# Two-pass scores on exact halves, rotary products shared between VectorE and GpSimd, and a range test by sums of squares, in a latent attention kernel

## The chip, the cores and the metric

The kernel runs on one core of one Trainium2 chip, in one launch. The metric is the device time in microseconds (us), the median of the runs; lower is better. Engines are named as in the profile: PE is TensorE (PEld its weight loads), DVE is VectorE, ACT is ScalarE, POOL is GpSimd, SP is SyncE, which here only issues DMAs.

## The reference, cut to what matters

Eight sequences (batches) of 1024 rows with 256 features go through a layer of latent attention and then through two layers of windowed attention with an MLP. The change touches the first layer alone. There are 16 heads of 16 dimensions; a rotary term of 32 dimensions is shared by all heads.

```python
c_kv = x @ W_kv_down
k_rope = _rotary_apply(c_kv @ W_k_rope, cos, sin)
k = (c_kv @ W_k_up).reshape(Bb, Tt, NH, HD)
v = (c_kv @ W_v_up).reshape(Bb, Tt, NH, HD)
q = (x @ W_q).reshape(Bb, Tt, NH, HD)
q_rope = _rotary_apply(x @ W_q_rope, cos, sin)
scores = jnp.einsum('bqhd,bkhd->bhqk', q, k)
scores = scores + jnp.einsum('bqr,bkr->bqk', q_rope, k_rope)[:, None]
scores = scores / scale
scores = jnp.where(causal[None, None], -jnp.inf, scores)
w = jax.nn.softmax(scores, axis=-1)
attn = jnp.einsum('bhqk,bkhd->bqhd', w, v).reshape(Bb, Tt, D_MODEL)
return attn @ W_o
```

The input x is normalised first, and the result is added to it. All data are float32.

## The kernel before, in words

The kernel has two stages. `mla` computes the first layer for the eight batches and leaves its result in DRAM (`x2d`); `local` computes the rest. A test at the end (`Verdict`) looks whether all values stayed in the range in which the short cuts of the kernel are exact; if not, a general version runs (it doesn't run here).

The exponential of the scores is split: exp(q k + rotary) = exp(q k) * exp(rotary). The rotary factor `er` is the same for all heads, so it is computed once for a block of queries and keys (`rotary`, L402 to L414), and each head's exp(q k) is multiplied by it (`turned`, L441 to L451).

Work in `mla` goes by units. A batch has 36 of them (list `units`, L571 to L577). A unit covers 512 columns for four heads, which is a block of 128 keys (or two narrower blocks at the causal border) for up to 512 queries c (c = 1 the later half of the queries, c = 0 the earlier) and a group g of four heads. For each unit:

- `scores` (L421): for each of the four heads a matmul over 32 rows of the array: `self.k[g]` (four heads of 32 rows) against `self.q`. Only 16 rows of 32 belong to one head: q holds two heads in 32 rows, and k is multiplied by a mask in `keys` (L372), so that the other head's rows are zero. The four matmuls lie in four row groups of the array. They fill two tiles `sc` in PSUM, and ACT takes the exponentials to two tiles `pt` of 128x1024 (L437), of six buffers.
- `turned` (L451): DVE multiplies both `pt` by `er`, which is broadcast over the heads.
- `values` (L453): four matmuls in four column groups add up v^T pt, with a column of ones in v for the sums; at the end of a row of units ACT copies the sum out, and `finished` and `turn_back` transpose and divide on DVE.

The order on PE, DVE, ACT and POOL is written out by hand (`manual_schedule`, L586 to L618). Step s issues the scores of unit s, the products of unit s - 1, the values of unit s - 2, and then the side work that the table `beside` (L513 to L556) gives to step s: for the same batch, the next one (1), the one after it (2) or the one before (-1). Side work is the projections of the next batch (`query`, `keys`, `value`, `down`, `rope_q`, `rope_k`), its normalisation and transposes, the rotary blocks and the output (`out_add`). A projection is summed by `dense` in one of two banks of PSUM (L324) and then copied out by ACT. Each engine works through its own list in order, so an instruction that waits holds up all behind it on the same engine. SP's order is not in the hand-written list: it issues loads of x, stores of x2d and, in the second stage, many DMAs.

`query` (L355) multiplies by wq, `keys` (L362) by wk; both are copies of the weights with columns put in the order in which two heads lie in 32 rows (L241 to L256). `rotary` takes two exponentials of each block, exp(+s) into `er` and exp(-s) back into PSUM, each with its sum along the row (`most`, `least`), for the range test at L620 to L623. A block at the causal border is cut to its triangle by POOL (L411). `rsqrt` (L125), a power on POOL, is the only other work of POOL in this stage.

In the second stage POOL works all the time: two operations of 128x1024 (L873 and L879) for each window, and selects. L956 and L1147 are DVE operations with two operands in SBUF.

Of the kernel before, what the change touches and what calls it, by code (L numbers as in the profile page):

```python
# [28 lines left out]

F32 = mybir.dt.float32  # L30
AF = mybir.ActivationFunctionType
ALU = mybir.AluOpType
AX = mybir.AxisListType
PSUM = bass.MemoryType.PSUM

P = 128
D = 256
T = 1024
# [15 lines left out]
TURN = 1e17  # L54
# [27 lines left out]
def preln_mla_local_kernel(  # L82
# [72 lines left out]
    def mla(ctx: ExitStack, verdict):  # L155
# [21 lines left out]
        def bank(name):  # L177
            if shared is None:
                return psum.tile([P, 512], F32, tag="mm", name=name)
            return two_banks(name)[:, 0, :]  # L180
# [59 lines left out]

        wq = wp.tile([P, 2, 2, 4, 2, HD], F32, name="wq")  # L241
        wk = wp.tile([P, 2, 4, 2, HD], F32, name="wk")
        mask = wp.tile([P, 2], F32, name="mask")
        for e in range(2):
            nc.vector.tensor_reduce(
                mask[:, e : e + 1], ident.rearrange("p (r e d) -> p r e d", e=2, d=HD)[:, :, e, :], AX.XY, ALU.add
            )
        for m in range(2):
            for e in range(2):
                cols = slice(128 * m + 64 * e, 128 * m + 64 * e + 64)  # L250
                nc.scalar.copy(
                    wq[:, :, m, :, e, :], wqnat[:, :, cols].rearrange("p c (r d) -> p c r d", d=HD)
                )
                nc.scalar.copy(wk[:, m, :, e, :], wknat[:, cols].rearrange("p (r d) -> p r d", d=HD))
        wq = wq.rearrange("p c m r e d -> p c m (r e d)")
        wk = wk.rearrange("p m r e d -> p m (r e d)")  # L256

        vs = []  # L260
# [7 lines left out]

        most = wp.tile([P, B * 12], F32, name="most")
        least = wp.tile([P, B * 12], F32, name="least")  # L270

        class Batch:


            def __init__(self, b):
                self.b = b
                self.sums = {}

# [23 lines left out]
            def normalise(self, n, part):  # L302
                mv, rstd = self.found[n]
                if part == 0:
                    if n == 0:
                        self.xn = []
                    self.xn.append(p1.tile([P, 4, D], F32, tag="xn", name=f"xn{self.b}_{n}", bufs=3))
                xn = self.xn[n]
                for i in (2 * part, 2 * part + 1):
                    nc.vector.tensor_scalar(  # L310
                        xn[:, i, :], self.x[:, 4 * n + i, :], mv[:, i, 0:1], rstd[:, i : i + 1],
                        ALU.subtract, ALU.mult,
                    )
# [34 lines left out]
            def rope_k(self, n, part=None):  # L348
# [3 lines left out]
                if ps is not None:  # L352
                    nc.vector.tensor_tensor(self.rk[:, HALF[n]], ps, tab[:, 1, HALF[n]], ALU.mult)

            def query(self, m, n, c, part=None):  # L355
                if m == 0 and n == 1 and c == 0 and not part:
                    self.q = of[self.b % 2].tile([P, 2, T], F32, tag="q", name=f"q{self.b}")
                ps = self.dense(f"psq{m}_", [wq[:, 0, m, :], wq[:, 1, m, :]], self.xnc, n, c, part)
                if ps is not None:
                    on_a(self.q[:, m, HALF[n]], ps)  # L360

            def keys(self, m, n, part=None):  # L362

                if n == 0 and not part:
                    if m == 0:
                        self.k = []
                    for e in range(2):
                        g = 2 * m + e
                        self.k.append(of[self.b % 2].tile([P, T], F32, tag=f"k{g}", name=f"k{self.b}_{g}"))
                ps = self.dense(f"psk{m}_", [wk[:, m, :]], [self.ckvT], n, 0, part)  # L370
                for e in range(2) if ps is not None else ():
                    nc.scalar.activation(  # L372
                        self.k[2 * m + e][:, HALF[n]], ps, AF.Identity, scale=mask[:, e : e + 1]
                    )

            def value(self, g, part=None):
# [25 lines left out]
            def rotary(self, c, kb):  # L402
                q0, w, er = self.block(c, kb)
                ps = bank(f"psR{self.b}_{c}_{kb}")
                times(ps[:, :w], self.rk[:, kb * P : (kb + 1) * P], self.rq[:, q0 : q0 + w], True, True)
                n = 12 * self.b + 8 * (1 - c) + kb
                nc.scalar.activation(er, ps[:, :w], AF.Exp, scale=SCALE, accum_out=most[:, n : n + 1])  # L407

                nc.scalar.activation(ps[:, :w], ps[:, :w], AF.Exp, scale=-SCALE, accum_out=least[:, n : n + 1])
                if q0 == kb * P:  # L410
                    nc.gpsimd.affine_select(  # L411
                        out=er[:, :P], in_=er[:, :P], pattern=[[1, P]],
                        compare_op=ALU.is_ge, fill=0.0, base=0, channel_multiplier=-1,
                    )  # L414

            def start(self):
# [4 lines left out]
            def scores(self, key, parts):  # L421
# [3 lines left out]
                for c, g, kb in parts:  # L425
                    q0, w, _ = self.block(c, kb)
                    for n in range(4):
                        rows = slice(32 * n, 32 * n + 32)
                        nc.tensor.matmul(  # L429
                            two[n // 2][:, n % 2, lo : lo + w], self.k[g][rows, kb * P : (kb + 1) * P],  # L430
                            self.q[rows, g // 2, q0 : q0 + w], start=True, stop=True,
                        )
                    lo += w
# [7 lines left out]
            def turned(self, parts, pts):  # L441
# [6 lines left out]
                er = er.unsqueeze(1)  # L448
                for pt in pts:
                    t = pt.rearrange("p j (s w) -> p (j s) w", w=w)  # L450
                    nc.vector.tensor_tensor(t, t, er.to_broadcast([P, 1024 // w, w]), ALU.mult)  # L451

# [21 lines left out]
            def finished(self, c, g, oT):  # L474


                nat = late.tile([P, 16, 32], F32, tag="onat", name=f"onat{self.b}_{c}_{g}", bufs=3)
                nc.vector.transpose(nat.rearrange("p b d -> p (b d)"), oT)
# [39 lines left out]
        for step, who, *what in (  # L518
# [21 lines left out]
            (21, 1, "rope_k", 1), (21, 1, "query", 0, 1, 0, 0),  # L540
            (22, 1, "query", 0, 1, 0, 1), (22, 1, "query", 0, 1, 1),
            (23, 1, "keys", 0, 0), (23, 2, "statistics", 0, 0),
            (24, 1, "value", 0),
            (25, 1, "value", 1),
            (26, 1, "keys", 0, 1), (26, 2, "statistics", 0, 1),
            (27, 1, "rotary", 1, 0),
# [72 lines left out]

        ok = small.tile([P, 2, B * 12], F32, tag="okr", name="okr", bufs=1)  # L620
        nc.vector.tensor_scalar(ok[:, 0, :], most, TURN, None, ALU.is_le)
        nc.vector.tensor_scalar(ok[:, 1, :], least, TURN, None, ALU.is_le)
        verdict.add(ok.rearrange("p m n -> p (m n)"), "turn")  # L623

# [1215 lines left out]
```

## Time and profile before

| What | us |
|---|---|
| median of three runs (3347.45 to 3350.44) | 3350.26 |
| the profiled execution, first to last instruction (span) | 3347.4 |
| first stores of x2d, batches 0 to 4 | 151.58, 272.93, 394.25, 515.59, 636.92 |
| last copy of a sum in the first stage (ACT, L78) | 1011.2 |
| one rotary product on DVE (128x1024, L451) | 1.217 |
| one exponential of scores on ACT (128x1024, L437) | 1.029 |
| busy in 272.9 to 394.3: PE, DVE, ACT, POOL | 120.4, 107.8, 96.9, 9.5 |
| mean granted clock of PE | 0.993 of full |

In the profile a group is one source line on one engine: out<-in with the names of tiles, then count, busy time, mean ns of one, and the idle time of the engine just before, with who ended it. An fp32 matmul leaves two records, each with its weight load. The chain of waits follows the work that ended last backwards. In a timeline each line has start, length, engine, source line, operation and count. Two operations that follow each other on DVE or ACT overlap by some hundredths of a microsecond, so that busy time is a little less than count times mean.

### The profile page before, as it was taken

How to read it: one execution, taken by the hardware profiler on the slowest of the kernel's cores; microseconds unless marked ns; L12 is line 12 of the kernel's file. 1: busy time of each engine (PE TensorE's matmuls, PEld its weight loads, DVE VectorE, ACT ScalarE, POOL GpSimd, SP SyncE). 2: the span in 40 equal slices, each digit the busy share in tenths (PEclk: the TensorE clock that was granted, in tenths of full speed). 3: DMA queues.
4: the chain of work that ended last, by engine and by line, in shares of the span. 5: the costliest groups of instructions: out<-in, count | busy, mean ns of one | idle time of the engine just before them, and what ended most of it. 6: DMA issues, size and time to landing. Idle time of an engine off the chain costs nothing.

```text
span 3347.4 us, 79461 instructions
## 1 busy us (share of the span) xinstructions
PE 3270.7 (98%) x33826; PEld 1777.5 (53%) x33826; DVE 2686.0 (80%) x3993; ACT 1713.1 (51%) x2238; POOL 1341.6 (40%) x1031
## 2 busy tenths in 40 slices
PE   8999999999987899999999999999999999999998
PEld 2433333333333556666565666566666566665665
DVE  5888888888897887888878887777878778787773
ACT  6878878877862244434444434444444444344441
POOL 1000000000006655655655555555555555555540
PEclk9999999999998899999999999999999999999999
DMA  1000000000032444445344354444545444454431
GB/s 63 8 20 27 8 20 27 8 20 14 14 105 81 115 114 120 123 115 143 105 121 127 113 136 130 137 127 136 134 134 139 121 126 130 124 148 119 109 107 58
DMA packets 369290, 311.74 MB, mean 93 GB/s; under 512 B 154607, under 2 KB 333214, under 8 KB 368798
## 3 DMA queue, kind: packets, MB, share of 16 engines
q1 hardware_dynamic: 366942, 304.16, 33.1%
q8 instruction: 268, 4.39, 0.6%
q10 hardware_dynamic: 1984, 2.41, 0.2%
q14 instruction: 96, 0.79, 0.1%
HBM read 165.96 MB, written 140.51 MB: 92 GB/s over the span
## 4 chain that ended last, share of the span: by engine, by line
PE 90%; DVE 3%; ACT 2%; DMA 1%; issue 1%; SPq 1%; POOL 1%; ACTq 0%; DVEq 0%
PE ag L1088 17%; PE pair L859 13%; PE sc L429 9%; PE psy L1129 8%; PE acc L462 8%; PE psw L1005 7%; PE o L972 6%; PE pv L886 6%; PE pair L931 4%; PE psq L200 2%; PE psx L200 2%; PE s L980 2%; PE psR L200 2%; DVE pt L451 1%; PE psy L1135 1%
## 5 line engine op out<-in xcount | busy, mean ns | idle before, releaser
L451 DVE TENSOR_TENSOR pt<-pt,er 128x1024 f32<-128x1024 f32 x576 | 674.8, 1217 | 77.8 <-ACT pt L437 77.8
L437 ACT ACTIVATE pt<-sc 128x1024 f32<-128x1024 f32 x576 | 560.7, 1029 | 174.0 <-PE sc L429 161.6
L1088 PE MATMUL ag<-d,l 128*128 128x512 f32 x1408 | 640.4, 597 | 1.2 <-DVE xs L1009 0.8
L873 POOL TENSOR_TENSOR t<-t,t 128x1024 f32<-128x1024 f32 x128 | 302.0, 2360 | 792.0 <-DVE t L869 792.0
L937 ACT ACT_TABLE_LOAD x120 | 154.0, 1283 | 702.0 <-PE pair L931 702.0
L859 PE MATMUL pair<-l_qkv,xT 128*128 128x512 f32 x1024 | 469.2, 601 | 5.5 <-DMA xT<-zx 2.4
L1088 PEld LDWEIGHTS ag<-d,l 128*128 128x128 f32 x1408 | 262.2, 190 | 310.2 <-issue 278.1
L125 POOL TENSOR_TENSOR rn<-ss,half 128x16 f32<-128x16 f32 x128 | 373.4, 2917 | 13.7
L429 PE MATMUL sc<-q,k 32*128 32x512 f32 (+3 forms) x3072 | 369.9, 522 | 5.1 <-ACT pt L437 5.0
L462 PE MATMUL acc<-pt,v 128*32 128x512 f32 (+3 forms) x3072 | 332.9, 496 | 4.8 <-DVE pt L451 4.6
L859 PEld LDWEIGHTS pair<-l_qkv,xT 128*128 128x128 f32 x1024 | 193.7, 192 | 248.8 <-issue 207.6
L864 ACT ACTIVATE sq<-pair 128x1024 f32<-128x1024 f32 x128 | 131.0, 1023 | 333.2 <-issue 269.1
L866 DVE TENSOR_TENSOR t<-pair,l_cos 128x1024 f32<-128x1024 f32 x128 | 156.2, 1220 | 157.4 <-ACT sq L864 156.7
L1129 PE MATMUL psy<-l,hid 128*128 128x256 f32 x1280 | 281.5, 379 | 0.0
L1101 DVE SCALAR_TENSOR_TENSOR hid<-ag,l_b,ge 128x512 f32<-128x512 f32 x160 | 115.9, 724 | 196.3 <-ACT ge L1100 171.3
L1129 PEld LDWEIGHTS psy<-l,hid 128*128 128x128 f32 x1280 | 243.2, 190 | 46.7 <-issue 15.1
L937 ACT ACTIVATE pt<-pair 128x1024 f32<-128x1024 f32 (+1 forms) x256 | 234.9, 968 | 56.7 <-PE pair L931 55.4
L429 PEld LDWEIGHTS sc<-q,k 32*128 32x128 f32 x3072 | 157.3, 184 | 199.9 <-ACT pt L437 154.3
L411 POOL TENSOR_SCALAR_AFFINE_SELECT er<-er 128x128 f32<-128x128 f32 x64 | 51.5, 804 | 524.0 <-ACT er L407 524.0
L879 POOL TENSOR_TENSOR t<-t,rn 128x1024 f32<-128x1024 f32 x128 | 249.2, 1947 | 10.0
L972 PEld LDWEIGHTS o<-pt,v 128*32 128x32 f32 x7680 | 201.6, 110 | 88.0 <-issue 82.0
L886 PE MATMUL pv<-l_qkv,xT 128*128 128x512 f32 x512 | 240.6, 592 | 0.0
(132 smaller groups left out, 4876.8 us busy)
## 6 DMA issues: line engine op xcount, KB each, us to landing
z<-turned SPq DMA_DIRECT2D x512, 128.0 KB, 2.4
qkT<-z SPq DMA_DIRECT2D x128, 512.0 KB, 3.7
y<-xs SPq DMA_DIRECT2D x128, 128.0 KB, 2.6
h<-y SPq DMA_DIRECT2D x32, 512.0 KB, 4.0
zx<-turneds SPq DMA_DIRECT2D x120, 128.0 KB, 2.7
xT<-zx SPq DMA_DIRECT2D x240, 64.0 KB, 2.6
zh<-turnedh SPq DMA_DIRECT2D x120, 128.0 KB, 2.3
d<-zh SPq DMA_DIRECT2D x30, 512.0 KB, 3.2
```

The costliest lines, as they stand in the source:

```text
L125: nc.gpsimd.tensor_tensor(out_, in_, half[:, :n], ALU.pow)
L429: nc.tensor.matmul(two[n // 2][:, n % 2, lo : lo + w], self.k[g][rows, kb * P : (kb + 1) * P], self.q[rows, g // 2, q0 : q0 + w], start=Tr ...
L437: nc.scalar.activation(pt, sc, AF.Exp, scale=SCALE)
L451: nc.vector.tensor_tensor(t, t, er.to_broadcast([P, 1024 // w, w]), ALU.mult)
L462: nc.tensor.matmul(self.acc[g][32 * n : 32 * n + 32, q0 - c * 512 :], self.v[:, kb, h * VW : h * VW + 32], pts[n // 2][:, n % 2, lo : lo + w],
L859: nc.tensor.matmul(qk[:, n].rearrange("p h d -> p (h d)"), self.left(i)[c], w["qkv"][:, c, n * INNER : (n + 1) * INNER], start=(c == 0), s ...
L873: nc.gpsimd.tensor_tensor(t1, t1, t2, ALU.add)
L886: nc.tensor.matmul(pv, self.left(i)[c], self.w["qkv"][:, c, 2 * INNER :], start=(c == 0), stop=(c == 1))
L937: nc.scalar.activation(pt[:, :, : n * P], flat[:, :, : n * P], AF.Exp, scale=-1.0)
L972: nc.tensor.matmul(o[32 * j : 32 * j + 32, g, a, :], vs[m][:, h * DH + a * 32 : h * DH + a * 32 + 32], pts[m][g][:, place(j), off : off + ...
L1088: nc.tensor.matmul(ps.rearrange("p (s a t) -> p s a t", a=4, t=32), w["1"][:, c, i, :], d[:, c], start=(c == 0), stop=(c == 1),)
L1129: nc.tensor.matmul(ps[:, t, :], hid[:, i, cols], w["2"][:, i, :], start=(t == i == 0), stop=False)
```

## The change

Four things change in the first stage.

1. Scores. `halves` takes a projection from PSUM, has ACT write it as float32r[...] and has DVE subtract that from the original: two halves whose sum is exact. Sixteen DMAs in SBUF put the halves where the matmuls need them: for k, the upper and the lower half of a head lie in the 16 + 16 rows of its row group; for q, both 16 rows hold the same head, and upper and lower half lie beside each other in columns. Two float32r matmuls, one for each half of q, then add up all four partial products. The copies of the weights and the mask are gone. The halves have two buffers; q and k are now tiles by group and by half of the sequence.
2. Rotary products. Of three units, two give the first of their two products to POOL: 192 of 576.
3. Range test. The second exponential and the row sums are gone. POOL squares rq and rk of a batch (`squares`), PE adds them over the rows (`reach`), and DVE takes the maximum.
4. Buffers: `xn` has two in place of three (the squares use them too), `onat` two in place of three.

The core of the diff:

```diff
-        wq = wp.tile([P, 2, 2, 4, 2, HD], F32, name="wq")
-        wk = wp.tile([P, 2, 4, 2, HD], F32, name="wk")
-        mask = wp.tile([P, 2], F32, name="mask")
...
-        most = wp.tile([P, B * 12], F32, name="most")
-        least = wp.tile([P, B * 12], F32, name="least")
+        norms = wp.tile([P, B], F32, name="norms")
+        ones = wp.tile([P, 32], F32, name="ones_m")
+        nc.gpsimd.memset(ones, 1.0)
...
+            def halves(self, ps, name):
+                t = p1.tile([P, 2, 512], F32R, tag="halves", name=f"{name}{self.b}", bufs=2)
+                on_a(t[:, 0], ps)
+                nc.vector.tensor_tensor(t[:, 1], ps, t[:, 0], ALU.subtract)
+                return t.bitcast(F32)
...
-                ps = self.dense(f"psq{m}_", [wq[:, 0, m, :], wq[:, 1, m, :]], self.xnc, n, c, part)
-                if ps is not None:
-                    on_a(self.q[:, m, HALF[n]], ps)
+                w = [wqnat[:, i, m * P : (m + 1) * P] for i in range(2)]
+                ps = self.dense(f"psq{m}_", w, self.xnc, n, c, part)
+                if ps is None:
+                    return
+                t = self.halves(ps, f"qh{m}{n}_")
+                for g in (2 * m, 2 * m + 1):
+                    q = of[g % 2].tile([P, 2, 512], F32, tag=f"q{g}{n}", name=f"q{self.b}_{g}_{n}")
+                    for s in range(8):
+                        lo = 64 * (g % 2) + HD * (s // 2)
+                        nc.sync.dma_start(q[HD * s : HD * s + HD], t[lo : lo + HD])
+                    self.q[g, n] = q.bitcast(F32R)
...
-                for e in range(2) if ps is not None else ():
-                    nc.scalar.activation(
-                        self.k[2 * m + e][:, HALF[n]], ps, AF.Identity, scale=mask[:, e : e + 1]
-                    )
+                t = self.halves(ps, f"kh{m}{n}_")
+                for g in (2 * m, 2 * m + 1):
+                    k = of[self.b % 2 if (m, n) == (0, 0) else 0].tile(
+                        [P, 512], F32, tag=f"k{g}{n}", name=f"k{self.b}_{g}_{n}"
+                    )
+                    for s in range(8):
+                        lo = 64 * (g % 2) + HD * (s // 2)
+                        nc.sync.dma_start(k[HD * s : HD * s + HD], t[lo : lo + HD, s % 2])
+                    self.k[g, n] = k.bitcast(F32R)
...
-                nc.scalar.activation(er, ps[:, :w], AF.Exp, scale=SCALE, accum_out=most[:, n : n + 1])
-
-                nc.scalar.activation(ps[:, :w], ps[:, :w], AF.Exp, scale=-SCALE, accum_out=least[:, n : n + 1])
+                nc.scalar.activation(er, ps[:, :w], AF.Exp, scale=SCALE)
...
+            def squares(self, n):
+                t = (self.rq, self.rk)[n]
+                sq = p1.tile([P, T], F32, tag="xn", name=f"sq{self.b}_{n}", bufs=2)
+                nc.gpsimd.tensor_tensor(sq, t, t, ALU.mult)
+                self.sq = getattr(self, "sq", []) + [sq]
+
+            def reach(self):
+                ps = bank(f"reach{self.b}")
+                for i, four in enumerate(QUARTER):
+                    nc.tensor.matmul(ps[four], ones, self.sq[i // 2][:, HALF[i % 2]], start=True, stop=True)
+                nc.vector.tensor_reduce(norms[:, self.b : self.b + 1], ps, AX.X, ALU.max)
...
-                    for n in range(4):
-                        rows = slice(32 * n, 32 * n + 32)
-                        nc.tensor.matmul(
-                            two[n // 2][:, n % 2, lo : lo + w], self.k[g][rows, kb * P : (kb + 1) * P],
-                            self.q[rows, g // 2, q0 : q0 + w], start=True, stop=True,
-                        )
+                    k = self.k[g, kb // 4][:, kb % 4 * P : (kb % 4 + 1) * P]
+                    q = self.q[g, c][:, :, q0 - c * 512 :]
+                    for h in (1, 0):
+                        for n in range(4):
+                            rows = slice(32 * n, 32 * n + 32)
+                            nc.tensor.matmul(
+                                two[n // 2][:, n % 2, lo : lo + w], k[rows], q[rows, h],
+                                start=(h == 1), stop=(h == 0),
+                            )
...
-                for pt in pts:
+                for i, pt in enumerate(pts):
                     t = pt.rearrange("p j (s w) -> p (j s) w", w=w)
-                    nc.vector.tensor_tensor(t, t, er.to_broadcast([P, 1024 // w, w]), ALU.mult)
+                    self.shared[0] += i == 0
+                    on = nc.gpsimd if i == 0 and self.shared[0] % 3 else nc.vector
+                    on.tensor_tensor(t, t, er.to_broadcast([P, 1024 // w, w]), ALU.mult)
...
-            (22, 1, "query", 0, 1, 0, 1), (22, 1, "query", 0, 1, 1),
-            (23, 1, "keys", 0, 0), (23, 2, "statistics", 0, 0),
+            (22, 1, "query", 0, 1, 0, 1), (22, 1, "query", 0, 1, 1), (22, 1, "squares", 0),
+            (23, 1, "keys", 0, 0), (23, 2, "statistics", 0, 0), (23, 1, "squares", 1),
...
-            (26, 1, "keys", 0, 1), (26, 2, "statistics", 0, 1),
+            (26, 1, "keys", 0, 1), (26, 2, "statistics", 0, 1), (26, 1, "reach"),
```

Where the side work fills halves: query(1,1) in step 1 (qh11), keys(1,0) in step 3 (kh10), keys(1,1) in step 4 (kh11), query(0,0) in step 5 (qh00), query(1,0) in step 10 (qh10), and for the next batch query(0,1) in step 22 (qh01), keys(0,0) in step 23 (kh00) and keys(0,1) in step 26 (kh01). The DMAs stand in SP's queue in this order, with stores of x2d after those of step 5 and loads of x after those of step 10.

## The prediction

> **What bounds the kernel now.** I read the busy rows of the page, then the busy times of single batches, the chain of waits inside one batch, the groups of the stage by shape, and the timelines of VectorE (DVE), GpSimd (POOL) and the SP queue.
>
> ```profile
> PE 3270.7 (98%) x33826; PEld 1777.5 (53%) x33826; DVE 2686.0 (80%) x3993; ACT 1713.1 (51%) x2238; POOL 1341.6 (40%) x1031
> ...
> PE   8999999999987899999999999999999999999998
> ...
> DVE  5888888888897887888878887777878778787773
> ...
> POOL 1000000000006655655655555555555555555540
> ```
>
> The change lies in the first 1011 us, the first twelve slices, where POOL shows 1 or 0. There PE is full and DVE is next.
>
> ```profile
> 272.90:394.30 121.40, 120.40 (x1304) 47.31 (x1298) 107.77 (x138) 96.93 (x150) 9.50 (x10) 1.00 0.06 19
> ```
>
> This is one batch: length, then busy PE, weight loads, DVE, ACT, POOL. The first stores of three batches go out at 151.58, 272.93 and 394.25, so a batch takes 121.3 us, and its 36 steps 3.37 us each.
>
> ```profile
> 289.22 1.29 PE sc L429 x8
> 290.52 1.00 PE acc L462 x8
> 291.51 0.86 PE psv L200 x16
> 292.38 1.07 PE sc L429 x8
> 293.45 1.00 PE acc L462 x8
> ```
>
> Inside a batch the chain never leaves PE: scores, values, one piece of side work. Some scores take 1.29 or more instead of 1.07; over a batch these excesses sum to some 5 us. They are PE's only waits, so PE needs about 116 of the 121.3 us.
>
> ```profile
> L451 DVE TENSOR_TENSOR pt<-pt,er 128x1024 f32<-128x1024 f32 x360 | 421.8, 1217 | 38.0 <-ACT pt L437 38.0
> ```
>
> ```profile
> L873 POOL TENSOR_TENSOR t<-t,t 128x1024 f32<-128x1024 f32 x128 | 302.0, 2360 | 792.0 <-DVE t L869 792.0
> ...
> L879 POOL TENSOR_TENSOR t<-t,rn 128x1024 f32<-128x1024 f32 x128 | 249.2, 1947 | 10.0
> ```
>
> The first line is from the groups of five batches (busy time, mean ns of one), the others from the page. A rotary product takes DVE 1.217 us (72 a batch); POOL's operations of that size, in the second stage, take 2.36 (a sum) and 1.95 us (a product). Whether both engines can work at once decides this case, and two places of the trace tell. First one product pair on DVE and a small select on POOL:
>
> ```profile
> 156.48 2.35 DVE L451 TENSOR_TENSOR pt<-pt,er 128x1024 f32<-128x1024 f32 x2
> ```
>
> ```profile
> 157.72 1.26 POOL L411 TENSOR_SCALAR_AFFINE_SELECT er<-er 128x128 f32<-128x128 f32 x1 [2.38 <-ACT er L407]
> ```
>
> The select needs 0.292 us at its fastest. Here it starts inside DVE's pair and ends at 158.98, 0.15 us after DVE's end at 158.83. Then the other way round, in the second stage:
>
> ```profile
> 2431.53 0.69 DVE L1147 TENSOR_TENSOR x<-xs,x 128x512 f32<-128x512 f32 x1
> 2432.14 0.68 DVE L1141 TENSOR_TENSOR xs<-psy,xs 128x512 f32<-128x512 f32 x1
> 2432.86 1.68 DVE L1147 TENSOR_TENSOR x<-xs,x 128x512 f32<-128x512 f32 x1
> ```
>
> ```profile
> 2431.64 2.35 POOL L879 TENSOR_TENSOR t<-t,rn 128x1024 f32<-128x1024 f32 x1
> ```
>
> L1147 adds two SBUF tiles: beside POOL's product it takes 1.68 us, not 0.69, and ends 0.55 after POOL's end at 2433.99. L1141, with one operand in PSUM, runs beside the same product at 0.68. So a DVE operation with two SBUF operands and a POOL operation take turns, and a waiting one saves about 0.14 us of its own duration (0.29 to 0.15, 0.69 to 0.55).
>
> ```profile
> 1292.22 1.75 SPq L902 DMA_DIRECT2D z<-turned  x4
> ```
>
> ```profile
> z<-turned SPq DMA_DIRECT2D x512, 128.0 KB, 2.4
> ```
>
> SP starts a DMA every 0.48 us or so (four in 1.75, the next begins 0.05 later), and such a DMA lands 2.4 us after its issue.
>
> [...] The trace shows two records for each fp32 matmul and no reduced one[...]. [...] Scores (row tiles) cost 1.07 us where the column-tiled psv, as many columns, costs 0.86[...].
>
> **The change, part by part, for one batch.** *Scores:* [...] a batch has 36 such blocks' worth of columns, so PE saves 36 x 0.43 = 15.5 us. Were the new type no quicker, it saves nothing; were only the narrow blocks not quicker, about 14. The norms' matmuls (L200 form, four of 512 columns side by side) add 0.86. PE then needs 116 - 15.5 + 0.9 = 101 us. It would be the bound no longer.
>
> *ACT:* the second exponential goes (12 a batch, by the rows of L409 6.2 us, both accumulator reads 5.4), and eight masked key copies of 0.69 become four of 0.59 (3.2): 97 - 15 = 82. It hides behind the rest.
>
> *DVE:* 24 of 72 products leave (29.2); eight subtractions PSUM minus SBUF come, priced as L346 (128x512, 0.69: 5.5), and one reduction of 0.6: 108 - 23 = 85 busy.
>
> *Port:* POOL gets 24 products. I price one at 2.35, as L873, whose two operands are read whole like pt and er here; L879, whose small factor is repeated element by element, is the lower end at 1.90 (undisturbed). A pair that shares the port takes 2.35 - 0.14 + 1.217 - 0.14 = 3.29; a pair on DVE alone stays 2.35. So 24 x 3.29 + 12 x 2.35 = 107.2. Others on the port: two squarings 2 x 2.21 = 4.4; L484 8 x 0.42 = 3.4; eight selects at 0.15 = 1.2; two L125 of 1.43 = 2.9. Sum 119.1 us, in place of 72 x 1.17 + about 9 = 93 before.
>
> *Port left idle:* DVE's other work (other rows of its groups 24.1, new 6.1: 30 us) can hide under a POOL product only in the two thirds of the steps that have one; the squarings stand ahead of the products of steps 22 and 23 and are counted above. A third, 10 us, leaves the port empty. Bounds: 0 if POOL always has the next product ready, 20 if DVE's waits for ACT's copies come on top.
>
> *DMAs:* 64 for q and 64 for k, 128 x 0.48 = 61 us of SP's queue, hidden but for one place. The halves have two buffers; in steps 1, 3, 4, 5 four are filled. The copy in step 5 (qh00) needs the DMAs of step 3 landed, which stand behind those of step 1: 32 x 0.48 + 2.4 = 17.8 us after step 1's subtraction, and four steps of 3.6 us give 14.4. ACT stands about 3.5 us, 4 with the wait of step 4; behind it stand the exponentials of step 6, and on DVE, behind the subtraction, the products of step 5. Bounds: 0 (queued products cover it), 8 (0.6 us a DMA). Stores of x2d and loads of x queue behind 16 DMAs (8 us); x has three buffers, so nobody waits.
>
> *At nothing:* the removed weight copies (PE's first transposes wait for xn until 9.9 us anyway), one buffer fewer for xn and onat (their writers and readers follow in order), the shorter final test.
>
> Batch: 119.1 + 10 + 4 = 133, that is +11.8; seven of them +83. The eighth has less side work and PE less cover there: +15. Before the first scores 24 DMAs must land (12 + 2.4 us), half of it behind the rotary blocks, whose second exponentials are gone: +5. The second stage is untouched. Sum +103: the profiled span 3347.4 becomes 3450; the median 3350.3 is 2.9 above that span, so 3453.
>
> **Rivals.**
> (a) *The port does not bind; faster.* If POOL's product costs 1.90, the port sums to 119.1 - 26 x 0.45 = 107; with no idle port and no DMA stall the batch is set by port and PE (101 + 5 waits): 108. Seven times -13, the last -5, start +5: -91, 3259. For: L879 is a product as well, L873 a sum, and two steps of finished exponentials may keep POOL fed. Against: er is streamed like L873's operands. It decides where port, idle time and stall fall under 121: at 1.90 that is once idle time and stall together are below 14 us, at 2.35 below 2 us.
> (b) *Cheap product, the rest as forecast:* 121 to 127 a batch, 3350 to 3400.
> (c) *DMA and copy waits in full:* SP's 0.6 us a DMA, 8 us of stall, 15 us of idle port: 142 a batch, +145 to +170, 3510. For: both copy and subtraction stand in queues that feed the products. Against: two steps of products can wait ready.
> (d) *The reduced type isn't quicker:* PE stays at 117, below the port's 133, and its waits grow by some 2 us a batch: 3470, inside the forecast.
>
> **Chances.** Forecast with (d) 0.52 (3400 to 3500); (c) 0.18 (3500 to 3570); (b) 0.15 (3343 to 3400), of which 0.04 is within 0.2%; (a) 0.15 (3255 to 3343), below the range. About 0.2% (7 us) is what a measurement of this kernel can tell from no change. Slower 0.81, within 0.04, faster 0.15. The range 3350 to 3540 leaves out (a) and the end of (c).
>
> **What would show it.** A shared product pair with DVE's part ending 1.08 us after POOL's end, and lasting over 2 us by the record; POOL's product at 2.3 us or more, longer where it waited; PE with waits for POOL or DVE in acc, and scores at 0.64 us; ACT's qh00 copy waiting for a DMA; batches 133 us apart. DVE products that stay at 1.22 beside POOL's, or batches under 121 us, would prove me wrong.

## The result and the profile after

The changed kernel takes 3552.97 us (median of 4 runs, 3546.46 to 3557.66) against 3348.9 for the kernel before beside it: 1.0608 times as long (95% interval 1.0593 to 1.0624), or 204 us more. The forecast was 3453 and the range ended at 3540. The direction was right, the size was half of the truth.

First the page: busy rows, slices, and shares of the chain of waits.

```profile
PE 3301.5 (93%) x33890; PEld 1790.8 (50%) x33890; DVE 2811.6 (79%) x3870; ACT 1646.3 (46%) x1910; POOL 1916.3 (54%) x1240
...
PE   6888879888888779999999999999999999999999
...
DVE  3889788898788878887887888778777887787773
...
POOL 2655556556465476555555555555555555555540
PEclk8999889999999889999999999999999999999999
...
PE 71%; DVE 17%; SPq 4%; issue 3%; ACT 3%; DMA 2%; POOL 1%; DVEq 0%; ACTq 0%; POOLq 0%
```

The last of these lines read, in the kernel before:

```profile
PE 90%; DVE 3%; ACT 2%; DMA 1%; issue 1%; SPq 1%; POOL 1%; ACTq 0%; DVEq 0%
```

In the first third PE is no longer full and POOL works at half, but DVE shows the same eights as before: no engine looks like the bound. The chain has left PE for DVE and for the SP queue. After the first third the rows are nearly as they were.

One batch from the windows (length, then busy PE, weight loads, DVE, ACT, POOL, then the granted clock):

```profile
331.98:478.95 146.97, 125.50 (x1307) 48.70 (x1304) 124.64 (x123) 89.00 (x111) 82.79 (x37) 0.91 0.28 58
```

A batch went from 121.4 to 147.0. PE's busy time rose although its scores became shorter. The same 3072 value matmuls (acc), before and after, on the page:

```profile
L462 PE MATMUL acc<-pt,v 128*32 128x512 f32 (+3 forms) x3072 | 332.9, 496 | 4.8 <-DVE pt L451 4.6
L477 PE MATMUL acc<-pt,v 128*32 128x512 f32 (+3 forms) x3072 | 440.8, 526 | 134.4 <-DVE pt L466 111.4
```

One of them takes little longer (496 and 526 ns), but together they keep PE busy for 108 us more, and PE stands idle before them for 134 us. Before, the matmuls of a unit mostly started together; now they start apart, as their products come, so that their times cover each other less: count times mean is 4.6 times the busy time before and 3.7 times after.

Where the 204 us lie, by the copies of finished sums (oaT, eight a batch):

| Part | before | after | more | forecast |
|---|---|---|---|---|
| start to the first score matmul | 31.2 | 45.7 | 14.5 | 5 |
| from there to the first sum | 56.8 | 67.6 | 10.8 | in the next row |
| first sum to that of seven batches on | 845.5 | 1018.6 | 173.1 | 83 |
| from there to the last sum | 77.7 | 83.5 | 5.8 | 15 |
| start to the last sum | 1011.2 | 1215.4 | 204 | 103 |

The second stage took 2340 us in place of 2336. The products, from the groups of the whole page:

```profile
L466 POOL TENSOR_TENSOR pt<-pt,er 128x1024 f32<-128x1024 f32 x192 | 546.0, 2854 | 311.4 <-ACT pt L450 311.0
L466 DVE TENSOR_TENSOR pt<-pt,er 128x1024 f32<-128x1024 f32 x384 | 688.6, 1827 | 27.1 <-ACT pt L450 27.0
```

The mean of 1827 ns on DVE hides two kinds: 1.21 us alone, and far more beside POOL. Two lines of the timelines show such a pair, DVE first:

```profile
414.83 3.38 DVE L466 TENSOR_TENSOR pt<-pt,er 128x1024 f32<-128x1024 f32 x1
```

```profile
412.24 4.89 POOL L466 TENSOR_TENSOR pt<-pt,er 128x1024 f32<-128x1024 f32 x2
```

POOL ends at 417.13 and DVE at 418.21, 1.08 later, which is the forecast number. In the whole trace 115 of the 123 DVE products of over 1.7 us end 1.06 to 1.10 us after a POOL product (median 1.083), and a POOL product that waited ends 2.23 us after DVE's (median of 132). So the two take turns, and the prices 2.35 and 3.29 a pair were right. "Port" in the forecast and the expectations is a name for these turns; the traces show the turns and not what lies behind them. I also laid all operations that take part (POOL's, and DVE's rotary products, onat and xn) over each other for two batches in the middle: the turns fill 119.0 us a batch (119.1 was forecast) and leave 27.8 empty (14 was forecast, stall included). **The error inside a batch is in the empty time.**

The largest gap, 7.5 us, comes at step 5. The SP queue, then ACT, then DVE:

```profile
351.33 10.01 SPq L358 DMA_DIRECT2D q<-qh  x16
361.44 20.70 SPq L372 DMA_DIRECT2D k<-kh  x32
```

```profile
363.44 0.58 ACT L79 CAST kh<-psk 128x512 fp32r<-128x512 f32 x1 [4.54 <-DMA k<-kh]
363.92 1.95 ACT L450 ACTIVATE pt<-sc 128x1024 f32<-128x1024 f32 x2
373.76 0.58 ACT L79 CAST qh<-psq 128x512 fp32r<-128x512 f32 x1 [7.89 <-DMA k<-kh]
```

```profile
374.38 0.69 DVE L345 TENSOR_TENSOR qh<-psq,qh 128x512 fp32r<-128x512 f32 x1 [6.94 <-DMA k<-kh]
```

SP issues one such DMA every 0.63 to 0.65 us. The 16 DMAs of kh10 begin at 361.44 and need 10.3 us, the last lands about 2 us later, at 373.8: that is when ACT may overwrite the buffer. DVE stands behind ACT for 6.94 us, and POOL, whose next product needs ACT's next exponential, for 9.52.

**Two theories.** T1: the turns of DVE and POOL set the loss, and the time that they leave empty comes from the order of the work. T2, the rival: the copies of the halves by DMA set it, through their two buffers, and sharing hardly matters. T3 came later: copy, subtraction and transfer cost by standing in the queues that feed the products, even without stall and sharing.

### The profile page after: what moved, and what is told of

It is laid out like the page before. It is cut to its first block, busy times and chain, and to the rows that moved or that the text cites. A ratio compares the mean times of both kernels' runs of the same rounds, so it can differ in the third digit from the quotient of the medians.

```text
span 3555.8 us, 81311 instructions
## 1 busy us (share of the span) xinstructions
PE 3301.5 (93%) x33890; PEld 1790.8 (50%) x33890; DVE 2811.6 (79%) x3870; ACT 1646.3 (46%) x1910; POOL 1916.3 (54%) x1240
## 4 chain that ended last, share of the span: by engine, by line
PE 71%; DVE 17%; SPq 4%; issue 3%; ACT 3%; DMA 2%; POOL 1%; DVEq 0%; ACTq 0%; POOLq 0%
PE ag L1102 16%; PE pair L873 12%; DVE pt L466 10%; PE psy L1143 8%; PE psw L1019 6%; PE o L986 6%; PE pv L900 6%; PE pair L945 4%; PE acc L477 4%; PE sc L442 2%; SPq L372 2%; PE s L994 1%; PE psx L201 1%; DVE onat L499 1%; SPq L358 1%
## 5 line engine op out<-in xcount | busy, mean ns | idle before, releaser
L466 POOL TENSOR_TENSOR pt<-pt,er 128x1024 f32<-128x1024 f32 x192 | 546.0, 2854 | 311.4 <-ACT pt L450 311.0
L466 DVE TENSOR_TENSOR pt<-pt,er 128x1024 f32<-128x1024 f32 x384 | 688.6, 1827 | 27.1 <-ACT pt L450 27.0
L477 PE MATMUL acc<-pt,v 128*32 128x512 f32 (+3 forms) x3072 | 440.8, 526 | 134.4 <-DVE pt L466 111.4
L126 POOL TENSOR_TENSOR rn<-ss,half 128x16 f32<-128x16 f32 x128 | 373.4, 2917 | 13.7
L442 PE MATMUL sc<-q,k 32*128 32x512 f32 (+3 forms) x3072 | 253.7, 397 | 52.6 <-ACT pt L450 49.4
L442 PEld LDWEIGHTS sc<-q,k 32*128 32x128 f32 x3072 | 137.6, 193 | 251.7 <-ACT pt L450 167.4
L477 PEld LDWEIGHTS acc<-pt,v 128*32 128x32 f32 x3072 | 90.5, 111 | 334.8 <-DVE pt L466 206.7
```

The lines of the kernel that those rows point to most:

```text
L126: nc.gpsimd.tensor_tensor(out_, in_, half[:, :n], ALU.pow)
L442: nc.tensor.matmul(two[n // 2][:, n % 2, lo : lo + w], k[rows], q[rows, h], start=(h == 1), stop=(h == 0),)
L466: on.tensor_tensor(t, t, er.to_broadcast([P, 1024 // w, w]), ALU.mult)
L477: nc.tensor.matmul(self.acc[g][32 * n : 32 * n + 32, q0 - c * 512 :], self.v[:, kb, h * VW : h * VW + 32], pts[n // 2][:, n % 2, lo : lo + w],
```

## The experiments

All times are medians; the ratio is against the kernel before beside it, with its 95% interval. A batch is the mean over the seven distances between first sums (before 120.8, after 145.5), or, where a window is shown, that window.

**1. All products on VectorE.**

```diff
-                    on = nc.gpsimd if i == 0 and self.shared[0] % 3 else nc.vector
+                    on = nc.vector
```

> The changed kernel with all rotary products on VectorE. T1 (the shared port, filled by GpSimd's products, sets most of the loss): the port sum falls from 119 to about 97 us a batch, VectorE's own list becomes the longest at about 114 us plus the turns it gives to squares, selects and powers (8) plus part of the DMA stall: 122 to 130 a batch, 3350 to 3420 in all. T2 (the copies of the halves by DMA, with two buffers, set the loss): sharing hardly matters, batches stay at 140 or more, 3490 to 3550.

Measured: 3433.53 us, 1.0253 (1.0236 to 1.0270); 131.5 a batch. T2 fell as it was put: sharing is worth 119 us of the changed kernel. But T1's own numbers were missed by 14 us, and the stall is all there:

```profile
ACT qh L79 <- DMA k<-kh: 30.4, 4, 8.0
```

This is from the waits over 420 us, about three batches (total, times, longest). The loss has a second part.

**2. Sharing alone,** in the kernel before.

```diff
-                for pt in pts:
+                for i, pt in enumerate(pts):
...
+                    on = nc.gpsimd if i == 0 and self.shared[0] % 3 else nc.vector
```

> The kernel before with sharing of the products alone: two of three units give one product to GpSimd. T1: port 107 for the products plus 8 for the rest, plus an idle port like that of the changed kernel (20 to 28): 135 to 143 a batch, 3460 to 3525. T2: without the copies by DMA the port is idle for 5 us at most, so a batch stays near TensorE's 121: 3345 to 3390.

Measured: 3419.0 us, 1.0210 (1.0193 to 1.0227). Between the two: without any DMA for halves, sharing costs 70.6 us. One batch:

```profile
340.00:469.30 129.30, 123.93 (x1300) 47.58 (x1296) 117.87 (x114) 96.80 (x151) 75.25 (x35) 1.00 0.05 18
```

Laid out in the same way, the turns fill 115.5 us of the 129.3 (the forecast's sum without the squarings is 114.7) and leave 13.9 empty. Here all 105 DVE products of over 1.7 us end about 1.08 us after a POOL product. So sharing costs by itself, with nine tenths of the time filled by the turns, and some 14 us stay empty even where no DMA disturbs.

**3. The range test alone,** in the kernel before.

```diff
-                nc.scalar.activation(er, ps[:, :w], AF.Exp, scale=SCALE, accum_out=most[:, n : n + 1])
-
-                nc.scalar.activation(ps[:, :w], ps[:, :w], AF.Exp, scale=-SCALE, accum_out=least[:, n : n + 1])
+                nc.scalar.activation(er, ps[:, :w], AF.Exp, scale=SCALE)
...
+                nc.gpsimd.tensor_tensor(sq, t, t, ALU.mult)
...
+                    nc.tensor.matmul(ps[four], ones, self.sq[i // 2][:, HALF[i % 2]], start=True, stop=True)
```

> The kernel before with the range test by sums of squares alone (and xn with two buffers). TensorE is the bound and gets 0.9 us more a batch, ScalarE loses 12 us it did not need, and two squarings on GpSimd hold VectorE for 2.2 us each. Both theories: 3340 to 3365, within 0.3% of before. Over 3380 would mean that the squarings in steps 22 and 23, or the two xn buffers, are a part of the loss that neither theory names.

Measured: 3352.21 us, 1.0013 (1.0006 to 1.0020), 121.3 a batch as before. ScalarE's busy time in one batch falls from 96.9 to 91.1 us, DVE's rises from 107.7 to 111.5 with the squarings, and neither matters, since TensorE remains the bound (120.6 of 121.3).

**4. A quarter of the DMAs.** The rows of the two halves alternate, so that one DMA of 64 rows replaces four of 16; which of the 32 rows of a head holds what doesn't matter to the matmul as long as q and k agree.

```diff
-                    for s in range(8):
-                        lo = 64 * (g % 2) + HD * (s // 2)
-                        nc.sync.dma_start(q[HD * s : HD * s + HD], t[lo : lo + HD])
+                    lo = 64 * (g % 2)
+                    for e in range(2):
+                        nc.sync.dma_start(q[e::2], t[lo : lo + 64])
```

(and the same for k)

> The changed kernel with the two halves in alternate rows of a row group (row 2d + e in place of 16e + d), so that 2 DMAs of 64 rows fill a tile in place of 8 of 16: 32 a batch in place of 128. T1: the port remains full, only the long stalls at steps 3 to 5 go: 3 to 6 us a batch, 3500 to 3530. T2: ScalarE's 12.7 us of waiting for DMAs a batch go and the start of the stage comes 12 us sooner: 133 to 135 a batch, 3430 to 3460.

Measured: 3464.68 us, 1.0349 (1.0331 to 1.0366), 88 us below the changed kernel. This is 5 us above T2's range and 35 below T1's. No wait of ACT or DVE for a DMA of the halves is left in the same 420 us; the first scores start 4.4 us sooner (41.3), the first sum is copied 20.9 us sooner (92.4). The turns fill 119.0 us a batch again, and leave 15.9 empty in place of 27.8.

**5. Both undone:** products on VectorE, 32 DMAs a batch.

> The changed kernel with both undone: all products on VectorE and 32 DMAs a batch in place of 128. T1 (sharing and the DMA stall are the whole loss): VectorE's list of about 115 us is the longest, a batch is 117 to 123, 3320 to 3370. T3 (the halves cost by themselves, since copy, subtraction and transfer stand in order in the queues that feed the products): 126 to 130 a batch, 3390 to 3430.

Measured: 3331.91 us, 0.9954 (0.9937 to 0.9970): faster than the kernel before. T3 falls. With both parts undone the whole loss is gone. Sharing costs 132.8 us here (experiment 4 less this one) and 119 with the stall; the 96 more DMAs a batch cost 101.6 here (experiment 1 less this one) and 88 beside sharing. So the two nearly add up: 234 us one at a time, 221 together. One batch:

```profile
340.00:461.10 121.10, 116.40 (x1312) 46.34 (x1304) 116.07 (x147) 88.61 (x111) 19.33 (x12) 1.00 0.28 71
```

The batch is as long as before, but for another reason: scores of 512 columns now take PE 0.67 us, not 1.07, while DVE's list has grown from 107.8 to 116.1 us by subtractions and by waits for POOL's squares. What PE won, DVE lost.

**6. Half the sharing:** one unit in three.

```diff
-                    on = nc.gpsimd if i == 0 and self.shared[0] % 3 else nc.vector
+                    on = nc.gpsimd if i == 0 and self.shared[0] % 3 == 1 else nc.vector
```

(with 32 DMAs a batch)

> The changed kernel with 32 DMAs a batch, and one unit in three shared in place of two. T1 with a port that is always short (each GpSimd product costs the same): half way between no sharing and two in three, about 3405. T1 with a threshold (GpSimd's products hide under VectorE's other work until that is used up): port sum 108, below VectorE's and TensorE's needs, so nearly the time without sharing, 3340 to 3380.

Measured: 3408.39 us, 1.0180 (1.0162 to 1.0198): 76 us above none shared, where two in three cost 133. So POOL's help isn't free at twelve products a batch either: the first twelve cost more than the next twelve. The first expectation has the right number, but not the right reason: the turns fill only 107 of 130 us here, so that their time isn't always short (the table further down shows what costs instead).

**7 and 8. The normalisation xn on ScalarE,** with sharing and without (32 DMAs a batch). In the changed kernel DVE's xn lasts 0.40 us alone and up to 2.55 beside a POOL product.

```diff
+                    self.nb = small.tile([P, 4], F32, tag="nb", name=f"nb{self.b}_{n}")
+                    nc.vector.scalar_tensor_tensor(self.nb, mv[:, :, 0], -1.0, rstd, ALU.mult, ALU.mult)
...
-                    nc.vector.tensor_scalar(
-                        xn[:, i, :], self.x[:, 4 * n + i, :], mv[:, i, 0:1], rstd[:, i : i + 1],
-                        ALU.subtract, ALU.mult,
-                    )
+                    nc.scalar.activation(
+                        xn[:, i, :], self.x[:, 4 * n + i, :], AF.Identity,
+                        bias=self.nb[:, i : i + 1], scale=rstd[:, i : i + 1],
+                    )
```

> The changed kernel with 32 DMAs a batch, sharing as it is, and the eight normalisations xn of a batch on ScalarE (activation with scale and bias) in place of VectorE. If xn takes turns with GpSimd (it lasted 0.40 us alone and up to 2.47 beside a GpSimd product), VectorE gains its 3.2 us and the waits behind: 3 to 6 us a batch, 3415 to 3440 against 3465. If those waits are hidden behind others, within 5 us of 3465.

> No sharing, 32 DMAs a batch, and the normalisations xn on ScalarE. If VectorE's list is the bound without sharing, it falls by 3.2 us less the small multiplication that replaces it: 2.5 us a batch, 20 us below the same kernel without this edit, 3300 to 3350. If TensorE or the order of the waits is the bound, no change (within 5 us), or slower if ScalarE's queue then holds the exponentials up.

Measured: 3472.42 us (1.0365, 1.0347 to 1.0382) with sharing, 8 us above experiment 4, where the intervals overlap; and 3343.94 us (0.9986, 0.9980 to 0.9993) without, 12 us above experiment 5. Neither gained. A line of the waits of the second kernel, over 420 us, names a suspect:

```profile
ACT xn L295 <- DVE nb L292: 12.3, 6, 3.8
```

The small product that ScalarE needs as its bias stands in DVE's queue behind the rotary products, and ScalarE waits for it with exponentials behind. In experiment 7 the same wait takes 28.5 of 420 us.

**9. A third place for the halves,** with sharing and 128 DMAs as in the changed kernel.

```diff
-                t = p1.tile([P, 2, 512], F32R, tag="halves", name=f"{name}{self.b}", bufs=2)
+                tag = "xn" if name.startswith("kh10") else "halves"
+                t = p1.tile([P, 2, 512], F32R, tag=tag, name=f"{name}{self.b}", bufs=2)
```

> The changed kernel, sharing and 128 DMAs a batch as they are, with a third place for the halves in the crowded steps: those of keys(1,0) in step 3 lie in a buffer of xn, which is free then. If the DMAs cost through the two buffers (the copy of step 5 waits until those of step 3 have landed), the long stall goes: 8 to 11 us a batch, 3465 to 3490, with a late start as in the changed kernel. If they cost because SP hands q and k over too late for the scores, or by their traffic, nothing goes: 3540 or more.

Measured: 3478.21 us, 1.0386 (1.0369 to 1.0404), 135.3 a batch in place of 145.5. So it takes both to make the stall, SP's 0.63 us for each of the 128 DMAs and only two buffers: with one more place, 128 DMAs a batch cost as little in the middle of the stage as 32 (135.5). What stays is the start: the first sum at 102.5, not 92.4 as with 32 DMAs.

**10. The bias worked out early,** on GpSimd just after the power (xn on ScalarE, no sharing, 32 DMAs a batch, as in experiment 8).

```diff
+                nb = small.tile([P, 4], F32, tag="nb", name=f"nb{b}_{n}")
+                nc.gpsimd.tensor_tensor(nb, mv[:, :, 0], rstd, ALU.mult)
+                nc.gpsimd.tensor_scalar(nb, nb, -1.0, None, ALU.mult)
```

> No sharing, 32 DMAs a batch, the normalisations xn on ScalarE, and the bias that they need worked out on GpSimd right after the power, several steps before it is wanted. If the loss of 12 us in the first try came from ScalarE's wait for that bias in VectorE's queue, this one gains what VectorE is spared: about 3 us a batch, 3305 to 3315. If ScalarE's longer list is what holds the exponentials up, 3330 or more.

Measured: 3333.23 us, 0.9954 (0.9937 to 0.9970). The suspect is confirmed: 10.7 of the 12 us come back. But the kernel only equals the one of experiment 5. DVE's busy time in a batch fell by 2.2 us (116.1 to 113.9) and the batch by 0.6, and the first sum comes 2.7 us later (88.9 for 86.2). In a batch DVE and POOL now stand idle together for 6.7 us in place of 4.9. ScalarE's longer list (88.6 to 91.8) is a candidate, which no run tests.

**11. No lower half:** ScalarE writes zeros in place of DVE's subtraction (32 DMAs, no sharing).

```diff
-                nc.vector.tensor_tensor(t[:, 1], ps, t[:, 0], ALU.subtract)
+                nc.scalar.mul(t[:, 1], ps, 0.0)
```

> No sharing, 32 DMAs a batch; the lower half is not computed: ScalarE writes zeros in place of VectorE's subtraction (so the scores lose the small parts of q and k). If VectorE's list is the bound without sharing, the eight subtractions of 0.68 us are worth 5 us a batch: 3290 to 3300. If TensorE's waits set the end, under 2 us a batch: 3315 to 3332.

Measured: 3290.07 us, 0.9822 (0.9805 to 0.9838).

```profile
340.00:454.80 114.80, 111.76 (x1308) 46.34 (x1304) 111.00 (x139) 91.59 (x119) 16.13 (x13) 1.00 0.29 75
```

Eight subtractions of 0.68 us are 5.4 us; DVE's busy time fell by 5.1, and the batch by 6.3 (121.1 to 114.8). That is what DVE's list as the bound would give. But the edit also takes DVE out of the chain from projection to transfer, which no run separates, and experiment 10 gained far less for what it took from the same list. This kernel is no candidate, since it leaves work out; it prices the work.

**12. The squares on ScalarE** too, on top of experiment 10.

```diff
-                nc.gpsimd.tensor_tensor(sq, t, t, ALU.mult)
+                nc.scalar.activation(sq, t, AF.Square)
```

> As the kernel with the early bias, with the two squarings of a batch on ScalarE too, so that GpSimd holds VectorE for selects and powers alone. If a squaring costs VectorE its whole 2.2 us, 4 us a batch less than that kernel: 3270 to 3285. If the squarings lie beside VectorE's operations on PSUM, or ScalarE's 2 us more a batch are on the path, no gain: within 5 us of that kernel.

Measured: 3318.18 us, 0.9909 (0.9892 to 0.9925), 15 us below experiment 10, between the two expectations. It computes all that the reference asks and is faster than the kernels before and after the change. One batch:

```profile
345.00:463.20 118.20, 113.38 (x1312) 46.44 (x1308) 110.56 (x139) 93.15 (x121) 10.48 (x14) 1.00 0.28 73
```

GpSimd does almost nothing here. Two squarings a batch taken from it are worth 2.2 us; they would have been worth 4.4, by the forecast's 2.2 us each, if DVE had stood still for all of each.

## Why the prediction was right in direction and half in size

**Scores: right.** From the start of a unit's scores to the next work on PE, before and after:

```profile
309.44 1.14 PE L429 MATMUL sc<-q,k 32*128 32x512 f32 x8
310.51 1.07 PE L462 MATMUL acc<-pt,v 128*32 128x512 f32 x8
```

```profile
455.85 0.74 PE L442 MATMUL sc<-q,k 32*128 32x512 f32 x8
456.52 1.07 PE L477 MATMUL acc<-pt,v 128*32 128x384 f32 x16
```

A unit of 512-column blocks costs PE 0.67 us in place of 1.07 (0.64 forecast); narrow ones, two to a unit, 0.68 to 0.73. That the new type would take half of the 0.86 us of psv, and the 0.21 by which scores exceed it would stay, was the author's estimate: no trace of before has a matmul of that type. Measured, a unit saves 0.40 of the 0.43 forecast. That the clock fell to 0.91 in the changed kernel's stage was not foreseen. It goes with the waits and not with the matmuls: the clock is 1.00 in experiments 5 and 12, which use the same ones.

**ACT and DVE busy: DVE right, ACT mis-sized without effect.** DVE's list without sharing is 116.1, where 85 plus 24 products of 1.217 gives 114. ACT is at 89.0, not 82: of the 11.6 us of exponentials and accumulator reads taken out, experiment 3 shows only 5.8 in busy time. The chain doesn't rest on ACT's sum.

**Port: right.** The sum of 119.1 was measured at 119.0, and the sign to look for ("DVE's part ending 1.08 us after POOL's end") at 1.08 us. That the sums agree to a tenth is in part luck: the measured one counts DVE's xn, which the forecast's list leaves out (117.2 without), and the forecast priced L125 with its waits (1.43, where it takes 1.01). The turns are the same in the experiments: DVE's rotary product has a median of 1.22 us and lasts up to 3.41 in the changed kernel's 420 us, up to 3.39 in a stretch of 140 us of experiment 2 and up to 3.40 in one of experiment 4. This term makes sharing a loss in this stage: each product given to POOL adds 0.94 us to the sum by the forecast, 1.0 by the table below, and the gain, DVE's other work hidden behind it, did not catch up at either dose (experiment 6).

**Port left idle: too small.** "A third, 10 us, leaves the port empty": measured 13.9 in experiment 2 and 15.9 in experiment 4, where no DMA stalls. The range's 20 covered it. The same laying out, for two batches in the middle, splits the empty time in two, in us a batch:

| Kernel | batch | filled by the turns | DVE alone, outside the turns | DVE and POOL both idle |
|---|---|---|---|---|
| forecast | 133 | 119.1 | 10 | 4 (the stall) |
| changed | 146.8 | 119.0 | 11.1 | 16.7 |
| 1, all products on DVE | 132.0 | 94.8 | 21.7 | 15.5 |
| 2, sharing alone | 129.3 | 115.5 | 10.8 | 3.0 |
| 4, 32 DMAs | 134.9 | 119.0 | 10.4 | 5.5 |
| 5, both undone | 121.1 | 94.7 | 21.5 | 4.9 |
| 6, half the sharing | 130.0 | 107.2 | 17.0 | 5.8 |
| 9, a third place | 135.1 | 119.2 | 10.8 | 5.1 |

The part that the forecast reckoned with, DVE's other work in steps without a POOL product, came out as forecast (10.4 to 11.1). What the 10 left out is time in which both engines wait though no DMA stalls, 3.0 us in experiment 2 and 5.5 in experiment 4: the bounds name it ("if DVE's waits for ACT's copies come on top"), the middle has it at nothing.

The table also says what sharing costs. From experiment 5 to 4 the time in turns grows by 24.3 us, 11.1 us more of DVE's work are hidden behind POOL, and 0.6 us of idling come on top: 13.8 us a batch. The first twelve products (5 to 6) add 12.5 us to the turns and hide 4.5, the next twelve add 11.8 and hide 6.6. So a product costs even where the turns leave time empty, since a DVE product that waits for its turn, as the one of 3.38 us above, holds up DVE's list.

Why both stand still is less sure. In the changed kernel, over 420 us:

```profile
POOL pt L466 <- ACT pt L450: 102.8, 24, 10.8
```

POOL has nothing to multiply for 103 of 420 us: it gets at most one product a step and waits for ACT's exponential, which waits for PE's scores, which stand on PE behind values that wait for earlier products. That this order makes the 3 to 5.5 us without a stall is argued from the waits; no run isolates it.

**DMA stall: the step that failed.** "128 x 0.48 = 61 us", "ACT stands about 3.5 us, 4 with the wait of step 4". SP takes 0.63 us for each, so the same sum, 32 DMAs and the landing, gives 22.5 us instead of 17.8 against the time that four steps give. ACT stood 7.9 us at step 5 and 4.5 to 5.4 at step 4, to which the forecast gave half a microsecond, and the empty time grew by 11.9 us a batch (27.8 less 15.9), where the forecast had 4. The 0.48 came from the SP row of the second stage, where the transfers have another shape; the 0.6 that I kept as the bound, an estimate, was near the measured price. Even the bound of 8 was too low, since both steps stand. Experiments 4 and 9 show it by both ways out: with fewer DMAs, or one more buffer, the time in which both engines are idle falls from 16.7 to 5.5 and 5.1 us, and either takes 10 us from a batch. Of the 13.7 us that the forecast missed in a batch, the stall is some 7, the idling without a stall 5.5, and DVE's work alone 1. Rival (c), which took this price and 15 us of empty port, came to 142 a batch and 3510 to 3570, and is what happened, with 145.5.

**Start: "half of it behind the rotary blocks", +5.** The first score came 14.5 us later, and with 32 DMAs a batch it is still 10.4 later (experiment 5, 41.6). But there the second unit's scores come at 45.5, against 46.1 before, and the first sum 1.8 us sooner (86.2): the rotary blocks, which stood between the first and the second scores before, now run for the most part ahead of the first, so the cover was there. What the +5 left out are the stalls of the first batch's own steps, the same term again: the first sum came 25.3 us later with 128 DMAs, and 4.4 with 32 (experiment 4), about what was forecast. The eighth batch, at +15, came out at +5.8.

**Left out of the sum: xn.** It isn't free beside POOL. The row of L293 over one batch:

```profile
L293 DVE TENSOR_SCALAR xn<-x,mv,rstd x8: 400/404/2552, 364.7 to 398.8; 128x256 f32<-128x256 f32 x8
```

Minimum, median, maximum in ns: it ends 0.15 us after POOL's end when it waited. It adds 1.8 us a batch to the time in turns. Whether freeing it would gain anything beside sharing stays open: experiment 7 gained nothing, but it had the bias in DVE's queue, which alone cost experiment 8 most of 12 us, and the early bias was not run with sharing.

**Range and chances.** The forecast held (c) at 0.18 and cut it at 3540. The terms for empty time and stall were both taken at the middle of their bounds; the first ended near its upper bound, the second beyond it.

**Still open:** why 2.2 us less on DVE brought 0.6 in experiment 10 when 5.1 brought 6.3 in experiment 11; and what makes both engines idle for 3 to 5.5 us without a stall. Every kernel with sharing gave POOL the first product of a unit; the second one, or another order of the lists, was not run, nor were the DMAs issued from another engine's queue.

## What to carry to other kernels

Before giving work to GpSimd, see in the trace which of VectorE's operations take turns with it, and add up both engines' turns: here an operation that takes GpSimd 2.35 us and VectorE 1.22 made that sum larger (119.0 us a batch in place of 94.7), and it could have helped only if VectorE had enough work outside the turns, ready at the right time. Add also the time in which both stand still. Price a transfer from a row of the same shape (0.48 us from another one here, 0.63 measured), and where a buffer is freed by the last of many small DMAs, count issue time times their number against the steps until the buffer is needed; here larger DMAs or one more buffer were worth the same in the middle of the stage (135.5 and 135.3 us a batch). When a change lightens the bound, the next list sets the time: what TensorE saved here, 0.40 us a unit, was worth nothing where VectorE paid for it with 8.3 us more a batch (experiment 5: 121.1 us a batch, 121.4 before).

## What the runs showed of the hardware that was not expected

- A DVE operation with one tensor input in SBUF and its output there (tensor_scalar, fp32, 128x256) also takes turns with GpSimd: 0.40 us alone, up to 2.55 beside it. When it waited, it ended 0.15 us after POOL's end. In the changed kernel's 420 us no DVE operation with one operand in PSUM was held (0.67 to 0.69 us each for 128x512).
- From issue to issue SP took 0.63 us for a DMA of 16 rows within SBUF, and 0.62 to 0.63 for one of 64 rows (medians, the changed kernel and experiment 4): 32 larger ones cost a quarter of the issue time of 128.
- A DMA can write every second row of SBUF (experiment 4): the 64-row transfers landed in 2.3 us (k, 128 KB) and 3.3 us (q, 256 KB), against 2.0 and 2.3 for the small ones.
- PE's mean granted clock was lower where PE waited more. Over stretches of 140 us it was 1.00 where PE was busy for 134 to 135 us (experiments 2, 5 and 12), 0.98 to 0.99 at 128 (experiment 6), 0.96 at 122 to 125 (experiment 4), and 0.90 to 0.94 at 119 (the changed kernel); experiment 1 lies lower, with 0.95 and 0.98 at 127 to 128. Whether the lower clock adds to the loss in turn was not tested.
